# Cross-attention with LayerNorm: scaling on ScalarE, casts at the head of the next slot, projection six slots behind

## Chip, cores and metric

The kernel runs on one core of one Trainium2 chip. The metric is the device time of one execution in microseconds (us). Three runs of the kernel before took 683.48, 687.57 and 688.61 us; their median is 687.57.

## What is computed

A cross-attention layer with a residual and a LayerNorm. x is 4 x 2048 x 512, the context is 4 x 77 x 512, there are 16 heads of 32, all in f32; the mask is over the 77 context rows. Cut to what matters:

```python
qs = (q @ wq).reshape(Bq, Lq, H, HD).transpose(0, 2, 1, 3)
ks_ = (k @ wk).reshape(Bq, Lk, H, HD).transpose(0, 2, 1, 3)
vs = (v @ wv).reshape(Bq, Lk, H, HD).transpose(0, 2, 1, 3)
scores = jnp.einsum('bhqd,bhkd->bhqk', qs, ks_) / jnp.sqrt(jnp.float32(HD))
scores = jnp.where(mask[:, None, :, :], -jnp.inf, scores)
attn_w = jax.nn.softmax(scores, axis=-1)
attn = jnp.einsum('bhqk,bhkd->bhqd', attn_w, vs)
attn = attn.transpose(0, 2, 1, 3).reshape(Bq, Lq, H * HD)
out = attn @ wo + q
mu = jnp.mean(out, axis=-1, keepdims=True)
var = jnp.mean((out - mu) ** 2, axis=-1, keepdims=True)
return (out - mu) / jnp.sqrt(var + EPS) * gamma + beta
```

Here q is x, and k and v are both the context.

## The kernel before, in words

The 8192 rows of x are 64 tiles of 128 rows; two tiles make a block (32 blocks), sixteen tiles share one of the 4 batches of context. Every matmul on f32 data is made of three in a reduced format: each operand is split into a high part (a cast) and a low part (the difference), and high x high, high x low and low x high are added in PSUM. So every operand costs a cast on ScalarE and a subtraction on VectorE or GpSimd. The names of the parts end in h and l: xth and xtl (x, transposed), qh and ql (queries), ah and al (the values' product), kbh and kbl (keys, in blocks), wqh, wql, woh, wol (weights).

After a head that loads and splits the weights and makes the keys, a software pipeline runs over slots u = 0, 1, 2, ... (L423 on). The order of each engine's instructions is the order of the calls written out there by hand; no scheduler changes it. Every engine, and SP as the queue that issues most of the DMAs, works through its own list in order; tiles of a pool with so many buffers make an instruction wait until the buffer is free. In slot u, with tile t = u:

- load_xT (L108, odd slots): DMAs xT of a block, once on SP into xtf (one buffer) and once on GpSimd's queue into xth (two buffers). load_x (L325) brings the rows of tile u-4 for the residual.
- shift and scale (L359, L363, odd slots): for tiles u-7 and u-6, LayerNorm's -mean/std (L361, VectorE) and then the scaling of the even tile on VectorE (L371) and of the odd tile on ScalarE (L373).
- scores (L237): 12 matmuls (L248) into four PSUM banks, then 16 masked minimum operations on VectorE (L251), one a head, which write into pbuf (three buffers).
- exps (L262): 16 exponentials on ScalarE (L265), one a head, each with its sum.
- split_xT (L118, even slots) and affine (L375, odd slots), both on GpSimd: the low part of xT (L121), and gamma and beta of two tiles (L377, L378).
- transp (L282): VectorE transposes pbuf of tile u-1 in 32 x 32 blocks (L286). regroup (L291, even slots) has twelve DMAs of 128 KB, issued by SP (L297), which put the weights of a block into the order that the values' product wants (PT).
- mask_bias and mask_nan (L225, L230) for the next batch, in the thirteenth and fourteenth slot of each sixteen.
- o_proj (L329): 12 matmuls (L337) for tile u-5. av (L300, even slots): 32 small matmuls (L306), the product of values of block (u-4)/2. values (L177), in slots 1 to 3: the values themselves.
- q_half (L124): 24 matmuls (L138) for half of the queries of a later block.
- stats (L340): VectorE adds the projection and the residual (L343) into o (four buffers), takes the statistics (L345, L350, L356), and GpSimd the power -1/2 (L357).
- av_evac (L314, even slots): ScalarE casts ah (L320, two), VectorE subtracts al (L321). q_evac (L144): the same for qh (L148) and ql (L149).
- normalise (L274): VectorE's reciprocal of the sums (L277), and GpSimd's product with it (L280).
- store (L380, even slots): SP issues the two stores of tiles u-8 and u-7 (L381).

When a batch begins, kblocks (L168) casts the new keys on ScalarE (L173) and subtracts on VectorE (L174), between scores and exps. All PSUM tiles take turns in one pool of eight banks, in the order of the calls. The last four tiles are scaled on VectorE with gamma and beta in two operations (L368, L369).

Of the kernel before, what the change touches and what calls it, by code (L numbers as in the profile page):

```python
# [9 lines left out]
F32R = mybir.dt.float32r  # L10
# [3 lines left out]
ALU = mybir.AluOpType  # L14
# [3 lines left out]
P = 128  # L18
# [3 lines left out]
NK = 77  # L22
# [18 lines left out]
def xattn_layernorm(  # L41
# [43 lines left out]
    stage_b = sb.tile([P, 2, NC_D, D], F32, tag="PT", name="stage_b")  # L85
    ctx_t = sb.tile([P, NC_D, NB * NK], F32, tag="B", name="ctx_t")
    ctx_f = [ctx_t[:, c] for c in range(NC_D)]
    ctx_s = [sb.tile([P, NC_D, NB * NK], F32R, tag=t, name=f"ctx_s{t}") for t in ("AH", "AL")]
    wvh = [sb.tile([P, D], F32R, tag="o", bufs=4, name=f"wvh{c}") for c in range(NC_D)]
    wv2 = [sb.tile([P, 2, D], F32R, tag=t, name=f"wvl{t}") for t in ("AH", "AL")]  # L90
    wvl = [wv2[c // 2][:, c % 2] for c in range(NC_D)]
# [15 lines left out]

    def load_xT(b):  # L108
        f = sb.tile([P, NC_D, BLK], F32, tag="xtf", bufs=1, name=f"xtf_{b}")
        h = sb.tile([P, NC_D, BLK], F32R, tag="xth", name=f"xth_{b}")  # L110
        nc.sync.dma_start(f, xT[b])
        if b == 1:
            nc.scalar.copy(h, f)
        else:
            nc.gpsimd.dma_start(h, xT[b])
        blk[b] = [h, f]

    def split_xT(b):  # L118
# [49 lines left out]
    def kblocks(b, ms=slice(0, NG)):  # L168
        for j in range(GH):
            q = slice(HD * j, HD * (j + 1))  # L170
            cs = slice(NK * j, NK * (j + 1))
            src = kct[q, ms, b, keys_of(j)]
            nc.scalar.copy(kbh[q, ms, cs], src)  # L173
            nc.vector.tensor_tensor(kbl[q, ms, cs], src, kbh[q, ms, cs].bitcast(F32), ALU.subtract)  # L174


    def values(r0):  # L177
        w = min(P, NB * NK - r0)
        pv = bank(f"pv_{r0}")
        n = 0  # L180
        for c in range(NC_D):
            for i, v in ((0, wvh), (0, wvl), (1, wvh)):
                nc.tensor.matmul(
                    pv[:w, :], ctx_s[i][:, c, r0 : r0 + w], v[c], start=(n == 0), stop=(n == 11)
                )
                n += 1
        vt = sb.tile([P, D], F32, tag="xr", bufs=3, name=f"vt_{r0}")
        nc.scalar.copy(vt[:w], pv[:w])
        for b in range(NB):
            lo, hi = max(r0, b * NK), min(r0 + w, (b + 1) * NK)  # L190
            for a, k0, k1, p0 in ((0, 0, NK, 0), (1, 0, NK - TAIL_K, 0), (1, NK - TAIL_K, NK, NK)):
# [45 lines left out]
    def scores(t):  # L237
        b = t // 2
        qh, ql = qd[b]
        mb = bat[t // TPB][0]  # L240
        pb = pbuf[t % NPB]
        rs = slice((t % 2) * P, (t % 2) * P + P)
        nm = nmax[t] = sb.tile([P, H], F32, tag="nm", bufs=3, name=f"nm_{t}")
        sums[t] = sb.tile([P, H], F32, tag="sum", bufs=3, name=f"sum_{t}")
        for g in range(NG):
            sc = bank(f"sc_{t}_{g}")
            for n, (a, k) in enumerate(((qh, kbh), (qh, kbl), (ql, kbh))):
                nc.tensor.matmul(sc[:, :GW], a[:, g, rs], k[:, g, :], start=(n == 0), stop=(n == 2))  # L248
            for h in range(GH * g, GH * g + GH):
                j = h % GH  # L250
                nc.vector.tensor_tensor_reduce(  # L251
                    pb[:, h // 2, (h % 2) * NK : (h % 2 + 1) * NK],
                    sc[:, j * NK : (j + 1) * NK],
                    mb[:, t % TPB, keys_of(h)],
                    -1.0,
                    3.0e38,
                    ALU.add,
                    ALU.min,
                    accum_out=nm[:, h : h + 1],
                )  # L260

    def exps(t, lo, hi):  # L262
        pb = pbuf[t % NPB]
        for h in range(lo, hi):
            nc.scalar.activation(  # L265
                pb[:, h // 2, (h % 2) * NK : (h % 2 + 1) * NK],
                pb[:, h // 2, (h % 2) * NK : (h % 2 + 1) * NK],
                AF.Exp,
                bias=nmax[t][:, h : h + 1],
                scale=-1.0,  # L270
                accum_out=sums[t][:, h : h + 1],
            )
# [86 lines left out]
    def shift(b):  # L359
        mv, rn = mvs[b], rns[b]  # L360
        nc.vector.scalar_tensor_tensor(rn[:, 1, :], mv[:, :, 0], -1.0, rn[:, 0, :], ALU.mult, ALU.mult)  # L361

    def scale(t):  # L363
        o = od[t]
        b, tt = divmod(t, 2)
        mv, rn = mvs[b], rns[b]
        if t >= NT - TAILV:
            nc.vector.scalar_tensor_tensor(o, o, mv[:, tt, 0:1], gam, ALU.subtract, ALU.mult)  # L368
            nc.vector.scalar_tensor_tensor(o, o, rn[:, 0, tt : tt + 1], bet, ALU.mult, ALU.add)  # L369
        elif tt == 0:  # L370
            nc.vector.tensor_scalar(o, o, rn[:, 0, tt : tt + 1], rn[:, 1, tt : tt + 1], ALU.mult, ALU.add)  # L371
        else:
            nc.scalar.activation(o, o, AF.Identity, bias=rn[:, 1, tt : tt + 1], scale=rn[:, 0, tt : tt + 1])  # L373

    def affine(t):  # L375
        o = od[t]
        nc.gpsimd.tensor_tensor(o, o, gam, ALU.mult)  # L377
        nc.gpsimd.tensor_tensor(o, o, bet, ALU.add)  # L378

    def store(t):  # L380
        nc.sync.dma_start(out[t * P : (t + 1) * P, :], od.pop(t))  # L381
# [12 lines left out]
        nc.tensor.matmul(pw, warm[:, :P], warm, start=True, stop=True)  # L394

    x0f = sb.tile([P, NC_D, BLK], F32, tag="xtf", bufs=1, name="xtf_0")
    x0h = sb.tile([P, NC_D, BLK], F32R, tag="xth", name="xth_0")
    x0l = sb.tile([P, NC_D, BLK], F32R, tag="xtl", name="xtl_0")
    blk[0] = [x0h, x0l]
    for c in range(NC_D):  # L400
# [19 lines left out]
    mask_bias(0)  # L420
    mask_nan(0)


    load_xT(2)
    for u in range(NT + 9):
        t = u
        odd = u % 2
        b = (u + 5) // 2
        if odd and b < NBLK:
            load_xT(b)  # L430
        if 0 <= u - 4 < NT:
            load_x(u - 4)
        if odd and 0 <= u - 7 < NT - TAILV:
            shift((u - 7) // 2)
            scale(u - 7)
            scale(u - 6)
        if t < NT:
            scores(t)
            if t % TPB == TPB - 1 and t + 1 < NT:
                kblocks((t + 1) // TPB)  # L440
            exps(t, 0, 16)
        b = (u + 4) // 2
        if not odd and 2 <= b < NBLK:
            split_xT(b)
        if odd and 0 <= u - 7 < NT - TAILV:
            affine(u - 7)
            affine(u - 6)
        if 0 <= u - 1 < NT:
            transp(u - 1)
            if not odd:  # L450
                regroup((u - 1) // 2)
        m, at_ = divmod(u, TPB)
        if at_ == TPB - 6 and m + 1 < NB:
            load_mask(m + 1)
        if at_ == TPB - 4 and m + 1 < NB:
            mask_bias(m + 1)
        if at_ == TPB - 3 and m + 1 < NB:
            mask_nan(m + 1)
        o = u - 5
        if 0 <= o < NT:  # L460
            o_proj(o)
        b = (u - 4) // 2
        if not odd and 0 <= b < NBLK:
            av(b)
        if 1 <= u <= 3:
            values((u - 1) * P)
        qs = [(1, 0), (1, 1)] if u == 0 else [divmod(u + 3, 2)]
        qs = [q for q in qs if q[0] < NBLK]
        for q in qs:
            q_half(*q)  # L470
        if 0 <= o < NT:
            stats(o)
        if not odd and 0 <= b < NBLK:
            av_evac(b)
        for q in qs:
            q_evac(*q)
        if u == 0:
            load_wo()
        if 2 <= u <= 3:
            split_wo(2 * u - 4)  # L480
            split_wo(2 * u - 3)
        if t < NT:
            normalise(t)
        if o >= NT - TAILV and o < NT and (o % 2 or o >= NT - 2):
            for f in (o,) if o >= NT - 2 else (o - 1, o):
                scale(f)
                store(f)
        if not odd and 0 <= u - 8 < NT - TAILV:
            store(u - 8)
            store(u - 7)  # L490


# [43 lines left out]
```

## Time and profile before

| What | us |
|---|---|
| the profiled execution | 684.65 |
| its span | 682.9 |
| median of three runs | 687.57 |
| L265, exponentials on ScalarE, 1024 with their read-outs | 352.4 + 192.0, overlapping |
| L251, masked minimum on VectorE, 1024 with their read-outs | 164.7 + 82.0, overlapping |
| L138, query matmuls, 3 x 512 | 148.8 + 145.1 + 144.9 |
| L280, normalise on GpSimd, 64 | 144.8 |
| L286, transpose on VectorE, 64 | 96.5 |
| L373, scaling on ScalarE, 30 | 24.5 |

The mean granted clock of TensorE was 0.954 of full speed. How to read the lines of the profile: a group of instructions has its line in the kernel, the engine (PE is TensorE, DVE VectorE, ACT ScalarE, POOL GpSimd, SPq the queue of SP), the operation, what it writes and reads, the count, then the busy time in us and the mean duration in ns of one, and the idle time before. A wait has who waited for whom, the total in us, how often, and the longest. A line of a timeline has the start in us from the span's start, the duration in us, and then the instruction; what stands in brackets is the idle time ahead of it and who ended it. "issue" there means that nothing in the trace shows what it waited for. Matmuls are pipelined: their durations overlap, so the distance of two starts says what one costs.

### The profile page before, as it was taken

Reading aid. Unit: us, or ns where it says so; the run is one execution under the profiler, and the core shown is the slowest. Engines: PE = TensorE matmul, PEld = TensorE weight load, DVE = VectorE, ACT = ScalarE, POOL = GpSimd, SP = SyncE. Lnnn points to the kernel's source line nnn. Section 1 sums busy time; section 2 is a strip of 40 time slices with the busy share of each in tenths; the row PEclk is TensorE's granted clock in tenths of the full one; section 3 lists DMA queues with packets and bytes.
Section 4 is the critical chain, followed back from the end, with each engine's and each line's share of the span. In section 5 each row is a group of like instructions: output and inputs, shape, how many; then the busy total and the mean of one; then the engine's idle time right before and its main releaser. Section 6 shows DMA issues by size and latency. Waiting matters only on the chain.

```text
span 682.9 us, 15297 instructions
## 1 busy us (share of the span) xinstructions
PE 596.2 (87%) x4190; PEld 492.5 (72%) x4190; DVE 566.9 (83%) x2661; ACT 468.1 (69%) x2263; POOL 431.3 (63%) x303
## 2 busy tenths in 40 slices
PE   8996899988799888879699999998699989898754
PEld 6975788866687777668588787886588777676533
DVE  4666778899988889779988888889998888799936
ACT  6687766867767686676677777776866876677710
POOL 5662476766676676557576666775766677666641
PEclk9998999999999999999899999999899999999887
DMA  8646877665567765566756666677746666755652
GB/s 291 217 139 151 236 178 216 179 163 176 163 196 216 217 166 161 169 192 189 216 145 180 190 198 192 194 212 217 208 111 187 198 190 190 216 155 150 161 154 108
DMA packets 68463, 126.11 MB, mean 185 GB/s; under 512 B 14746, under 2 KB 16282, under 8 KB 68378
## 3 DMA queue, kind: packets, MB, share of 16 engines
q1 hardware_dynamic: 62954, 107.31, 55.3%
q0 software_dynamic: 5424, 17.83, 9.6%
q8 instruction: 34, 0.56, 0.3%
q14 instruction: 51, 0.42, 0.2%
HBM read 57.36 MB, written 16.78 MB: 109 GB/s over the span
## 4 chain that ended last, share of the span: by engine, by line
PE 31%; DVE 24%; ACT 20%; SPq 10%; DMA 7%; issue 5%; POOL 2%; POOLq 0%; DVEq 0%; ACTq 0%
ACT pbuf L265 17%; PE pq L138 11%; PE po L337 11%; SPq L297 9%; PE sc L248 6%; DMA out<-o 5%; DVE o L371 3%; DVE pbuf L251 3%; PE pa L306 3%; DVE ql L149 3%; DVE st L345 2%; DVE o L343 2%; DVE B L286 2%; DVE al L321 2%; DVE kbl L174 2%
## 5 line engine op out<-in xcount | busy, mean ns | idle before, releaser
L265 ACT ACTIVATE pbuf<-pbuf,nm 128x77 f32<-128x77 f32 x1024 | 352.4, 347 | 130.8 <-DVE nm L251 130.8
L280 POOL TENSOR_TENSOR pbuf<-pbuf,ri 128x1232 f32<-128x1232 f32 x64 | 144.8, 2262 | 158.9 <-DVE nm L251 97.3
L265 ACT ACTIVATION_READ_ACCUMULATOR pbuf<-pbuf,nm 128x1 f32 x1024 | 192.0, 188 | 0.0
L251 DVE CUSTOM_DVE_ANT_0 pbuf<-sc,mb 128x77 f32<-128x77 f32 x1024 | 164.7, 229 | 0.0
L138 PE MATMUL pq<-xth,wqh 128*128 128x256 f32 x512 | 148.8, 291 | 4.8 <-DVE ql L149 4.2
L138 PE MATMUL pq<-xtl,wqh 128*128 128x256 f32 x512 | 145.1, 283 | 1.8 <-POOL xtl L121 1.7
L138 PE MATMUL pq<-xth,wql 128*128 128x256 f32 x512 | 144.9, 283 | 0.5 <-DVE wql L98 0.4
L337 PE MATMUL po<-woh,ah 128*128 128x512 f32 x256 | 109.2, 427 | 33.1 <-ACT ah L320 27.7
L337 PE MATMUL po<-woh,al 128*128 128x512 f32 x256 | 108.9, 425 | 11.1 <-DVE al L321 11.1
L138 PEld LDWEIGHTS pq<-xth,wqh 128*128 128x128 f32 x512 | 98.1, 192 | 20.9 <-DVE ql L149 11.0
L337 PE MATMUL po<-wol,ah 128*128 128x512 f32 x256 | 105.9, 414 | 0.0
L286 DVE STREAM_TRANSPOSE B<-pbuf 128x1280 f32<-128x1280 f32 x64 | 96.5, 1507 | 5.7 <-POOL pbuf L280 5.6
L138 PEld LDWEIGHTS pq<-xtl,wqh 128*128 128x128 f32 x512 | 97.7, 191 | 3.9 <-POOL xtl L121 2.0
L138 PEld LDWEIGHTS pq<-xth,wql 128*128 128x128 f32 x512 | 97.7, 191 | 1.2 <-DVE wql L98 1.2
L248 PE MATMUL sc<-kbl,qh 128*128 128x308 f32 x256 | 80.0, 312 | 12.5 <-DVE kbl L174 12.5
L337 PEld LDWEIGHTS po<-woh,ah 128*128 128x128 f32 x256 | 51.6, 202 | 48.1 <-ACT ah L320 39.3
L343 DVE TENSOR_TENSOR o<-po,xr 128x512 f32<-128x512 f32 x64 | 43.0, 672 | 51.1 <-DMA out<-o 22.3
L121 POOL TENSOR_TENSOR xtl<-xtf,xth 128x1024 fp32r<-128x1024 f32 x31 | 74.5, 2404 | 16.0 <-DMA xtf<-xT 9.5
L251 DVE DVE_READ_ACCUMULATOR2_ANT nm<- 128x1 f32 x1024 | 82.0, 80 | 0.0
L248 PE MATMUL sc<-kbh,qh 128*128 128x308 f32 x256 | 79.8, 312 | 1.6 <-DVE nm L251 0.9
L378 POOL TENSOR_TENSOR o<-o,bet 128x512 f32<-128x512 f32 x60 | 77.9, 1298 | 4.7
L377 POOL TENSOR_TENSOR o<-o,gam 128x512 f32<-128x512 f32 x60 | 78.8, 1314 | 2.8 <-DVE o L371 2.2
(75 smaller groups left out, 944.1 us busy)
## 6 DMA issues: line engine op xcount, KB each, us to landing
PT<-B SPq DMA_DIRECT2D x384, 128.0 KB
xr<-x SPq DMA_DIRECT2D x64, 256.0 KB
out<-o SPq DMA_DIRECT2D x64, 256.0 KB
xtf<-xT SPq DMA_DIRECT2D x31, 512.0 KB
xth<-xT POOLq DMA_DIRECT2D x30, 512.0 KB, 4.7
stage_a<-wq SPq DMA_DIRECT2D x4, 256.0 KB
stage_a<-wk SPq DMA_DIRECT2D x4, 256.0 KB
stage_b<-wv SPq DMA_DIRECT2D x4, 256.0 KB
```

What stands on the lines that cost most here:

```text
L121: nc.gpsimd.tensor_tensor(l, f, h.bitcast(F32), ALU.subtract)
L138: nc.tensor.matmul(pq[:, i * BLK : (i + 1) * BLK], w[:, c, ms], r[:, c, :], start=(n == 0), stop=(n == 11))
L248: nc.tensor.matmul(sc[:, :GW], a[:, g, rs], k[:, g, :], start=(n == 0), stop=(n == 2))
L251: nc.vector.tensor_tensor_reduce(pb[:, h // 2, (h % 2) * NK : (h % 2 + 1) * NK], sc[:, j * NK : (j + 1) * NK], mb[:, t % TPB, keys_of(h)], ...
L265: nc.scalar.activation(pb[:, h // 2, (h % 2) * NK : (h % 2 + 1) * NK], pb[:, h // 2, (h % 2) * NK : (h % 2 + 1) * NK], AF.Exp, bias=nmax[t ...
L280: nc.gpsimd.tensor_tensor(pv, pv, rv.to_broadcast((P, NP, 2, NK)), ALU.mult)
L286: nc.vector.transpose(bts[b][:, :, :, tt, :].rearrange("p c q r -> p q c r"), pbuf[t % NPB].rearrange("p q (c r) -> p q c r", c=5),)
L297: nc.sync.dma_start(pt[32 * c : 32 * c + 32, i], src[32 * i : 32 * i + 32])
L337: nc.tensor.matmul(po, a[:, c, rs], w[:, c, :], start=(n == 0), stop=(n == 11))
L343: nc.vector.tensor_tensor(o, pos.pop(t), xr.pop(t), ALU.add)
L377: nc.gpsimd.tensor_tensor(o, o, gam, ALU.mult)
L378: nc.gpsimd.tensor_tensor(o, o, bet, ALU.add)
```

## The change

It does the following. Both tiles of a pair are scaled on ScalarE, and L371 is gone. The casts and subtractions of the queries and of the values' product leave the end of the slot and come at the head of the next one: behind the scores, ahead of kblocks, scale and exps. The projection runs six slots behind the scores instead of five, and what follows it moves along: loads of x at u-5, LayerNorm of tiles u-8 and u-7 in even slots, stores of tiles u-9 and u-8 in odd slots. Loads of xT come at the head of even slots and their splits in odd slots; split_xT(2) comes at the end of slot 0. xth has three buffers. The values are made in slots 1 (two parts) and 2 (one part) instead of 1, 2 and 3, and the split context that they and the keys read lies in the buffers with the tag B instead of AH and AL. mask_nan moves from the fourteenth to the fifteenth slot of sixteen.

```diff
-    ctx_s = [sb.tile([P, NC_D, NB * NK], F32R, tag=t, name=f"ctx_s{t}") for t in ("AH", "AL")]
+    ctx_2 = sb.tile([P, 2, NC_D, NB * NK], F32R, tag="B", name="ctx_s")
+    ctx_s = [ctx_2[:, i] for i in range(2)]
...
-        h = sb.tile([P, NC_D, BLK], F32R, tag="xth", name=f"xth_{b}")
+        h = sb.tile([P, NC_D, BLK], F32R, tag="xth", bufs=3, name=f"xth_{b}")
...
-        elif tt == 0:
-            nc.vector.tensor_scalar(o, o, rn[:, 0, tt : tt + 1], rn[:, 1, tt : tt + 1], ALU.mult, ALU.add)
         else:
             nc.scalar.activation(o, o, AF.Identity, bias=rn[:, 1, tt : tt + 1], scale=rn[:, 0, tt : tt + 1])
...
+    evac = []
...
-    for u in range(NT + 9):
-        t = u
+    for u in range(NT + 8):
         odd = u % 2
-        b = (u + 5) // 2
-        if odd and b < NBLK:
+        o = u - 6
+        b = (u + 6) // 2
+        if not odd and 3 <= b < NBLK:
             load_xT(b)
-        if 0 <= u - 4 < NT:
-            load_x(u - 4)
-        if odd and 0 <= u - 7 < NT - TAILV:
-            shift((u - 7) // 2)
-            scale(u - 7)
-            scale(u - 6)
-        if t < NT:
-            scores(t)
-            if t % TPB == TPB - 1 and t + 1 < NT:
-                kblocks((t + 1) // TPB)
-            exps(t, 0, 16)
-        b = (u + 4) // 2
-        if not odd and 2 <= b < NBLK:
-            split_xT(b)
-        if odd and 0 <= u - 7 < NT - TAILV:
-            affine(u - 7)
-            affine(u - 6)
+        if 0 <= u - 5 < NT:
+            load_x(u - 5)
+        ln = [f for f in (u - 8, u - 7) if not odd and 0 <= f < NT - TAILV]
+        if ln:
+            shift(ln[0] // 2)
+        if u < NT:
+            scores(u)
+        if odd and 0 <= (u - 5) // 2 < NBLK:
+            av_evac((u - 5) // 2)
+        for q in evac:
+            q_evac(*q)
+        if u < NT and u % TPB == TPB - 1 and u + 1 < NT:
+            kblocks((u + 1) // TPB)
+        for f in ln:
+            scale(f)
+        if u < NT:
+            exps(u, 0, 16)
         if 0 <= u - 1 < NT:
             transp(u - 1)
             if not odd:
                 regroup((u - 1) // 2)
...
+        b = (u + 5) // 2
+        if odd and 3 <= b < NBLK:
+            split_xT(b)
+        for f in ln:
+            affine(f)
...
-        if at_ == TPB - 3 and m + 1 < NB:
+        if k == TPB - 2 and m + 1 < NB:
             mask_nan(m + 1)
-        o = u - 5
         if 0 <= o < NT:
             o_proj(o)
         b = (u - 4) // 2
         if not odd and 0 <= b < NBLK:
             av(b)
-        if 1 <= u <= 3:
-            values((u - 1) * P)
-        qs = [(1, 0), (1, 1)] if u == 0 else [divmod(u + 3, 2)]
-        qs = [q for q in qs if q[0] < NBLK]
-        for q in qs:
+        for r in {1: (0, P), 2: (2 * P,)}.get(u, ()):
+            values(r)
+        evac = [(1, 0), (1, 1)] if u == 0 else [divmod(u + 3, 2)]
+        evac = [q for q in evac if q[0] < NBLK]
+        for q in evac:
             q_half(*q)
         if 0 <= o < NT:
             stats(o)
-        if not odd and 0 <= b < NBLK:
-            av_evac(b)
-        for q in qs:
-            q_evac(*q)
         if u == 0:
             load_wo()
+            split_xT(2)
...
-        if not odd and 0 <= u - 8 < NT - TAILV:
+        if odd and 0 <= u - 9 < NT - TAILV:
+            store(u - 9)
             store(u - 8)
-            store(u - 7)
```

More of the change, by code (lines that the diff above doesn't have):

```diff
@@ L396, in xattn_layernorm @@
     x0f = sb.tile([P, NC_D, BLK], F32, tag="xtf", bufs=1, name="xtf_0")
-    x0h = sb.tile([P, NC_D, BLK], F32R, tag="xth", name="xth_0")
+    x0h = sb.tile([P, NC_D, BLK], F32R, tag="xth", bufs=3, name="xth_0")
     x0l = sb.tile([P, NC_D, BLK], F32R, tag="xtl", name="xtl_0")
@@ L451, in xattn_layernorm @@
                 regroup((u - 1) // 2)
-        m, at_ = divmod(u, TPB)
-        if at_ == TPB - 6 and m + 1 < NB:
+        b = (u + 5) // 2
[3 more added lines that the diff above has]
+            affine(f)
+        m, k = divmod(u, TPB)
+        if k == TPB - 6 and m + 1 < NB:
             load_mask(m + 1)
-        if at_ == TPB - 4 and m + 1 < NB:
+        if k == TPB - 4 and m + 1 < NB:
             mask_bias(m + 1)
-        if at_ == TPB - 3 and m + 1 < NB:
+        if k == TPB - 2 and m + 1 < NB:
             mask_nan(m + 1)
-        o = u - 5
         if 0 <= o < NT:
@@ L481, in xattn_layernorm @@
             split_wo(2 * u - 3)
-        if t < NT:
-            normalise(t)
+        if u < NT:
+            normalise(u)
         if o >= NT - TAILV and o < NT and (o % 2 or o >= NT - 2):
```

## The prediction

> **What bounds the kernel now.** I read the busy shares of the page first, then the granted clock, the groups by cost, the waits, and last the timelines of two slots around 357 to 374 us.
>
> ```profile
> PE 596.2 (87%) x4190; PEld 492.5 (72%) x4190; DVE 566.9 (83%) x2661; ACT 468.1 (69%) x2263; POOL 431.3 (63%) x303
> ...
> L371 DVE TENSOR_SCALAR o<-o,rn 128x512 f32<-128x512 f32 x30 | 74.5, 2484 | 1.4
> ```
>
> No engine is full. The second line is the operation that the change takes off VectorE: 2.48 us, four times the 0.67 us of an addition of the same shape (L343). Its fastest instance took 0.545 us and most take 2.62 us, beside the 2.26 us of GpSimd's L280.
>
> ```profile
> ACT pbuf L265 <- DVE nm L251: 130.8, 63, 4.6
> ...
> ACT o L373 <- DVE rn L361: 41.1, 29, 6.0
> ...
> PE po L337 <- ACT ah L320: 27.7, 19, 3.7
> ...
> DVE o L343 <- DMA out<-o: 22.3, 9, 7.2
> ```
>
> ScalarE waits for VectorE in each of 63 slots, TensorE for ScalarE: a ring, not a full engine.
>
> ```profile
> 366.31 0.69 DVE L345 BATCH_NORM_STATS2 st<-o 128x6 f32<-128x512 f32 x1
> ...
> 367.25 0.16 DVE L356 TENSOR_TENSOR rn<-mv,nz 128x2 f32<-128x2 f32 x1
> 368.05 1.29 DVE L321 TENSOR_TENSOR al<-pa,ah 128x512 fp32r<-128x512 f32 x2 [0.64 <-ACT ah L320]
> 369.26 0.68 DVE L149 TENSOR_TENSOR ql<-pq,qh 128x512 fp32r<-128x512 f32 x1
> ...
> 370.16 2.63 DVE L371 TENSOR_SCALAR o<-o,rn 128x512 f32<-128x512 f32 x1
> ...
> 375.24 1.50 DVE L286 STREAM_TRANSPOSE B<-pbuf 128x1280 f32<-128x1280 f32 x1
> ```
>
> The same stretch on ScalarE:
>
> ```profile
> 367.45 1.05 ACT L320 CAST ah<-pa 128x512 fp32r<-128x512 f32 x2
> 368.40 0.58 ACT L148 CAST qh<-pq 128x512 fp32r<-128x512 f32 x1
> ...
> 373.03 0.36 ACT L265 ACTIVATE pbuf<-pbuf,nm 128x77 f32<-128x77 f32 x1 [2.06 <-DVE nm L251]
> ```
>
> ScalarE casts ah and qh only after its sixteen exponentials; VectorE waits for them, subtracts, scales for 2.63 us, and only then feeds the next exponentials, which start 5.6 us after the last ones ended.
>
> ```profile
> 357.22 0.30 PE L248 MATMUL sc<-kbh,qh 128*128 128x308 f32 x1
> ...
> 358.91 0.40 PE L337 MATMUL po<-woh,ah 128*128 128x512 f32 x1
> ...
> 361.80 1.93 PE L306 MATMUL pa<-PT,vsb 96*32 96x256 f32 x32
> ...
> 363.66 0.39 PE L138 MATMUL pq<-xth,wqh 128*128 128x256 f32 x1
> ...
> 366.58 0.30 PE L248 MATMUL sc<-kbh,qh 128*128 128x308 f32 x1
> ...
> 374.08 0.30 PE L248 MATMUL sc<-kbh,qh 128*128 128x308 f32 x1
> ```
>
> Here TensorE ran a pair of slots without a stall: 374.08 - 357.22 = 16.86 us. The mean pair is longer. Slots by the starts of L280: the eighth at 100.27, the last at 648.52; 548.25 us for 28 pairs, 19.58 each. Of the 2.7 us between them, L371 holds 2.6.
>
> ```profile
> 441.52 7.64 SPq L297 DMA_DIRECT2D PT<-B  x12
> ...
> 449.89 0.89 SPq L381 DMA_DIRECT2D out<-o  x2
> ```
>
> and on VectorE:
>
> ```profile
> 454.14 0.69 DVE L343 TENSOR_TENSOR o<-po,xr 128x512 f32<-128x512 f32 x1 [1.66 <-issue]
> ```
>
> A second limit lies in the odd slots: the store stands on SP behind twelve regrouping issues, lands some 3.3 us after its own issue ended, and VectorE's L343 needs the freed o buffer in the very next slot.
>
> **The change, part by part.**
>
> *Scaling.* Thirty L371 of 2.48 us leave VectorE (74.5 us); thirty more activations like L373 (0.82 us) join ScalarE. An even slot then holds two of them in a row; two casts overlap by about 0.1 us (1.05 for twice 0.575), so I take 1.55 us per pair of slots. The Trainium skill ("ScalarE: Activation LUTs", Rules for kernel authors) says to give multiplications and additions to VectorE, not ScalarE. Going by that rule and by VectorE's 0.545 us, this part would lose 28 x (0.82 - 0.55) = 8 us. The rows decide otherwise: with GpSimd busy the same operation holds VectorE 2.62 us.
>
> *Casts at the head.* Same counts: 64 L148, 64 L320 and their subtractions. On ScalarE they now stand ahead of the exponentials, so a new wait arises: qh waits for the query matmuls of the slot before, TensorE's last there, and two scalings and sixteen exponentials queue behind it. On VectorE al and ql follow the sixteen L251, ahead of the transpose and the statistics. I walk both rings, with starts from the rows above. Even slot: from L361 to the scaling 0.14 (370.01 to 370.15), two scalings 1.55, exponentials 5.50 (361.95 to 367.45), end and reciprocal 0.26: 7.45. Odd slot, on VectorE: L251 2.52, al 1.21, ql 0.60, transpose 1.43, addition 0.69, statistics 0.73 and 0.21, then L356, the power on GpSimd and L361, about 1.0 as that power is now awaited (L356 at 367.25; the power took 367.49 to 368.20): 8.4. Ring: 15.85 us per pair. TensorE: 16.86. So TensorE becomes the bound, by 1.0 us only. The wait of qh costs nothing while the exponentials end inside TensorE's slot: start of scores + 0.3 + 0.57 + 1.55 + 5.50 = 7.9 of 9.36 us in an even slot; if that cover of 1.4 us goes, the excess lengthens each pair. TensorE in turn waits for the moved subtractions: by the turn of the eight banks, the query matmuls of an odd slot take the bank that the first al frees, at about 0.65 + 2.52 + 0.6 = 3.8 us of the slot, and come at 1.7 + 2.9 = 4.6; in an even slot it is ql, 3.8 against 6.4. Both are hidden by 0.8 us or more.
>
> *Projection six slots behind.* ah and al are ready a slot early, so TensorE's waits for them go (27.7 + 11.1 us on PE); next to be late is its own order. The last slot to project is number 69 instead of 68. In the drain TensorE idles anyway (16.4 us busy of the 30 from 650 us on), the last value product keeps its place, and al then goes ahead of the statistics of tile 61 instead of behind: I take 0, between -1.5 and one more projection of 2.8.
>
> *Issues moved.* SP: the load of xT goes from the head of odd to the head of even slots, x one slot later; stores go from behind the regrouping of the even slot to the end of the odd slot after it (again behind that slot's regrouping), and L343 wants their buffer only after the next transpose, so transpose to landing is 7.64 + about 0.8 + 1.0 + 3.3 = 12.7 of now a full pair, 16.9. That second limit goes, with 4 us to spare. The regrouping has landed about 6.2 + 7.6 + 2.1 = 15.9 us after the even slot starts (2.1 from the last issue's end, 660.33, to the matmul at 662.47); its matmul comes at 16.9 + 4.6 = 21.5. On GpSimd the split of xT (2.4 us) changes to odd and the affine steps to even slots; its ring is power 0.72, normalise 2.26, issue of xth 0.62, four affine steps 5.4, normalise 2.26, transpose and statistics on VectorE 3.2: 14.5 of 16.9. xth (median 4.7 us to land) is issued 3.7 us into the even slot, the split wants it at about 11.8: 3.4 us of cover. Third xth buffer and ctx_s in tag B: no time of their own.
>
> *Batch switches, masks.* Three times TensorE stood 5.2 us for kbl, and then ran at half the clock: pitch 0.255 us instead of 0.14. The two slots around 341.65 took 23.2 us, 4 above a pair. kbl took 4.25 us beside the affine steps of GpSimd; in the new order GpSimd is about to wait for the power, and kbl falls between 0.4 and 4.25 us. VectorE has 1.0 of slack: 0 to 3.3 us each; I take 1.5, nearer the lower end, as GpSimd is mostly idle there. Masks (1.85 and 1.75 us) now both fall in even slots, where VectorE needs 6.2 of 7.45: under 0.7 us, three times each, inside the slack: 0.
>
> *Clock.* The granted clock fell to 0.83 between 420 and 430 us, where TensorE had idled 1.64 us; the projections then ran 0.43 instead of 0.23 us apart for 3.4 us. The Trainium skill ("TensorE: Matmul & The Clock Gate", What's actually happening) puts the drop after an idle window of about 3.4 us. By that page the new order never drops. By the row a gap of 1.6 us can be enough, at some 1.7 us each; I take none in steady slots and leave five (8 us) to the range.
>
> *Head.* Up to the eighth slot SP paces both: 16 issues of vsb (17.7 us) and two regroupings. The first value matmuls wait for the same landing near 72 us. 0, between -3 and +3.
>
> *Sum.* Pair: 16.86 plus two restarts of about 0.1 (a first matmul after a wait takes 0.39, not 0.28): 17.1. 28 x 17.1 + 3 x 1.5 = 483 for 548: -65. The profiled execution took 684.65 us (span 682.9), so 684.65 - 65 = 620. The median of the three runs, 687.57, is 2.9 higher; I stay with the profiled one.
>
> **Rivals.**
> *The ring stays the bound.* It has only 1.0 us of distance, with some ten hand-overs whose price in the new order I can't see; 0.2 to 0.3 each brings 17.9 to 18.9. At 18.2: 28 x 18.2 + 4.5 = 514, -34: 651. For it: 130.8 us of waits of ScalarE for VectorE. Against: the starts I summed contain the hand-overs.
> *The gain is hidden anyway.* If the late landings set the pair (regrouping issues took 8.97 instead of 7.64 us at 262.57, and DMA's busy share would rise from 0.66 to 0.77), it stays near 19.4: 28 x (19.58 - 19.4) = 5 less: 680. Against: 4 us of cover.
> *Slower.* L361 now stands at the head of VectorE's even slot and waits for the power, which on GpSimd stands behind the split of xT. If xth lands late, L361 holds all sixteen L251, the scalings and the exponentials. The split ends 3.3 us ahead of the power; 1.0 more is the ring's slack; to lose, a pair must pass 19.6, another 2.7. xth would need 4.7 + 3.4 + 3.3 + 1.0 + 2.7, near 15 us instead of 4.7, in nearly every pair; at 16.6, 1.5 us x 28 = 42 more: 727. For it: xT's landing was already waited for, twice, up to 5.8 us. Against: only twice in 31.
>
> **How the numbers follow.** TensorE the bound: 0.58, own range 605 (pair 16.86, head and drain 5 shorter) to 633 (five clock drops 8, switches at 3.3 each 5 more). Ring: 0.26, 633 to 668. Hidden: 0.07, near 680. Slower: 0.09. The range 605 to 662 holds the first and most of the second, 0.8. A measurement here tells 1% (7 us) from no change: faster 0.85, same 0.06, slower 0.09.
>
> **What would show it.** L371 gone and 60 activations at about 0.82; pairs of L280 near 17.1; TensorE above 91% busy with a clock above 0.97; no wait of L337 for ah, none of L343 for out; kbl under 2 us at the switches. Wrong, if ScalarE still waits over 2 us a slot for VectorE, if L148 at the head waits so long that exponentials end after TensorE's slot, or if L361 waits for the power more than 1 us.

## The result and the profile after

The changed kernel took 654.82 us (median of four runs, 654.69 to 655.74), the kernel before 688.09 (four runs, 683.48 to 689.30): a ratio of 0.953, 95% interval 0.949 to 0.958. The forecast was 620. So the change is faster, by about half of what was forecast, and the question is where the other 35 us are. Ratios leave out single runs that were more than 1.5% above the fastest of the same kernel: one of the nine with the scaling alone, and one of the kernel before beside it.

The page of the changed kernel (its helpers stand one line lower: L361 is L362 now, L280 is L281, L251 is L252; L373 is L372): the busy times, and the shares of lines in the chain that ended last.

```profile
PE 580.5 (89%) x4190; PEld 489.9 (75%) x4190; DVE 550.9 (84%) x2631; ACT 483.7 (74%) x2293; POOL 431.3 (66%) x303
...
DVE 53%; ACT 23%; PE 10%; issue 5%; POOL 4%; SPq 3%; DMA 2%; DVEq 0%; POOLq 0%; ACTq 0%
ACT pbuf L266 19%; DVE pbuf L252 12%; DVE rn L362 10%; DVE B L287 8%; DVE al L322 5%; PE pq L139 5%; DVE st L346 4%; POOL rn L358 4%; DVE o L344 3%; DVE ql L150 3%; ACT o L372 3%; SPq L298 2%; PE pa L307 1%; DVE kbl L175 1%; DVE nm L252 1%
...
L372 ACT ACTIVATE o<-o,rn 128x512 f32<-128x512 f32 x60 | 45.7, 808 | 106.9 <-DVE rn L362 106.9
```

Sixty activations of 0.81 us, as priced. But the chain is VectorE's and ScalarE's, not TensorE's, and third in it, with 10% of the span, stands L362: an operation on 128 x 2 numbers. The waits of the changed kernel (who waited for whom: total us, times, longest):

```profile
ACT o L372 <- DVE rn L362: 106.9, 30, 4.7
...
DVE rn L362 <- POOL rn L358: 20.1, 30, 0.8
...
ACT pbuf L266 <- DVE nm L252: 8.1, 4, 7.5
```

ScalarE's 130.8 us of waiting for the minima in 63 slots have become 106.9 us of waiting for L362 in 30. L362 itself waits only 0.67 us each for the power. The wait is not where the time is; the operation is. Its instances in the kernel before and in the changed one (min/median/max in ns):

```profile
L361 DVE SCALAR_TENSOR_TENSOR rn<-mv,rn x30: 94/96/148, 91.6 to 655.2; 128x2 f32<-128x2 f32 x30
```

```profile
L362 DVE SCALAR_TENSOR_TENSOR rn<-mv,rn x30: 160/2206/2212, 104.5 to 623.8; 128x2 f32<-128x2 f32 x30
```

The same instruction on the same 256 pairs of numbers took 0.096 us before and takes 2.2 us now. The timelines of a pair of slots show why. VectorE, changed kernel:

```profile
361.06 0.16 DVE L357 TENSOR_TENSOR rn<-mv,nz 128x2 f32<-128x2 f32 x1
361.14 0.24 DVE L278 RECIPROCAL ri<-sum 128x16 f32<-128x16 f32 x1
362.05 2.20 DVE L362 SCALAR_TENSOR_TENSOR rn<-mv,rn 128x2 f32<-128x2 f32 x1 [0.66 <-POOL rn L358]
...
371.34 0.25 DVE L278 RECIPROCAL ri<-sum 128x16 f32<-128x16 f32 x1 [1.01 <-ACT pbuf L266]
371.51 0.18 DVE L252 CUSTOM_DVE_ANT_0 pbuf<-sc,mb 128x77 f32<-128x77 f32 x1
...
373.98 1.28 DVE L322 TENSOR_TENSOR al<-pa,ah 128x512 fp32r<-128x512 f32 x2
...
377.21 0.65 DVE L344 TENSOR_TENSOR o<-po,xr 128x512 f32<-128x512 f32 x1
...
378.84 0.16 DVE L357 TENSOR_TENSOR rn<-mv,nz 128x2 f32<-128x2 f32 x1
...
379.83 2.21 DVE L362 SCALAR_TENSOR_TENSOR rn<-mv,rn 128x2 f32<-128x2 f32 x1 [0.67 <-POOL rn L358]
```

GpSimd and ScalarE in the same stretch:

```profile
361.30 0.71 POOL L358 TENSOR_TENSOR rn<-rn,mhalf 128x2 f32<-128x2 f32 x1 [2.78 <-DVE rn L357]
361.99 2.24 POOL L281 TENSOR_TENSOR pbuf<-pbuf,ri 128x1232 f32<-128x1232 f32 x1
```

```profile
364.29 1.52 ACT L372 ACTIVATE o<-o,rn 128x512 f32<-128x512 f32 x2 [3.36 <-DVE rn L362]
365.71 0.34 ACT L266 ACTIVATE pbuf<-pbuf,nm 128x77 f32<-128x77 f32 x1
...
371.21 1.04 ACT L321 CAST ah<-pa 128x512 fp32r<-128x512 f32 x2
```

The power ends at about 362.0 and releases L362. At the same moment GpSimd starts its next instruction, the normalise of 2.24 us, whose reciprocal has been ready since 361.4. L362 ends when the normalise ends; sixteen minima on VectorE, two scalings and sixteen exponentials on ScalarE stand behind it. The same place in the kernel before, GpSimd's rows and VectorE's in order of time:

```profile
367.49 0.71 POOL L357 TENSOR_TENSOR rn<-rn,mhalf 128x2 f32<-128x2 f32 x1 [0.96 <-DVE rn L356]
370.24 2.26 POOL L280 TENSOR_TENSOR pbuf<-pbuf,ri 128x1232 f32<-128x1232 f32 x1 [2.04 <-DVE rn L361]
```

```profile
369.86 0.24 DVE L277 RECIPROCAL ri<-sum 128x16 f32<-128x16 f32 x1
370.01 0.09 DVE L361 SCALAR_TENSOR_TENSOR rn<-mv,rn 128x2 f32<-128x2 f32 x1
370.16 2.63 DVE L371 TENSOR_SCALAR o<-o,rn 128x512 f32<-128x512 f32 x1
```

There the casts' subtractions and the reciprocal stood between L356 and L361, so the power was long done; L361 came directly behind the reciprocal, in 0.09 us, and the normalise started after it. Then it was L371 that ran beside the normalise, for 2.63 us. The change took L371 off VectorE and put L362 in its place.

The Trainium skill ("SBUF — State Buffer", Who interferes with whom) has the rule: a VectorE instruction with two inputs in SBUF contends with a GpSimd instruction that reads SBUF, and the later one blocks until the other has ended. L362 reads mv and rn, both there. The rows agree: 2.20 us beside 2.24 us, 0.096 without. They also show the price for an instruction this small: the other one's whole length.

### The profile page after: what moved, and what is told of

It reads as the page before. It is cut to its first block, busy times and chain, and to the rows that moved or that the text cites. A ratio compares the mean times of both kernels' runs of the same rounds, so it can differ in the third digit from the quotient of the medians.

```text
span 652.9 us, 15185 instructions
## 1 busy us (share of the span) xinstructions
PE 580.5 (89%) x4190; PEld 489.9 (75%) x4190; DVE 550.9 (84%) x2631; ACT 483.7 (74%) x2293; POOL 431.3 (66%) x303
## 4 chain that ended last, share of the span: by engine, by line
DVE 53%; ACT 23%; PE 10%; issue 5%; POOL 4%; SPq 3%; DMA 2%; DVEq 0%; POOLq 0%; ACTq 0%
ACT pbuf L266 19%; DVE pbuf L252 12%; DVE rn L362 10%; DVE B L287 8%; DVE al L322 5%; PE pq L139 5%; DVE st L346 4%; POOL rn L358 4%; DVE o L344 3%; DVE ql L150 3%; ACT o L372 3%; SPq L298 2%; PE pa L307 1%; DVE kbl L175 1%; DVE nm L252 1%
## 5 line engine op out<-in xcount | busy, mean ns | idle before, releaser
L266 ACT ACTIVATION_READ_ACCUMULATOR pbuf<-pbuf,nm 128x1 f32 x1024 | 194.9, 190 | 0.0
L281 POOL TENSOR_TENSOR pbuf<-pbuf,ri 128x1232 f32<-128x1232 f32 x64 | 144.0, 2251 | 55.5 <-DVE ri L278 51.0
L252 DVE CUSTOM_DVE_ANT_0 pbuf<-sc,mb 128x77 f32<-128x77 f32 x1024 | 164.9, 230 | 13.2 <-PE sc L249 13.2
L372 ACT ACTIVATE o<-o,rn 128x512 f32<-128x512 f32 x60 | 45.7, 808 | 106.9 <-DVE rn L362 106.9
L338 PE MATMUL po<-woh,ah 128*128 128x512 f32 x256 | 106.7, 417 | 7.5 <-DVE o L344 5.6
L338 PE MATMUL po<-woh,al 128*128 128x512 f32 x256 | 105.4, 412 | 2.5 <-DVE al L322 2.5
L358 POOL TENSOR_TENSOR rn<-rn,mhalf 128x2 f32<-128x2 f32 (+1 forms) x33 | 24.5, 743 | 111.7 <-DVE rn L357 111.7
L249 PE MATMUL sc<-kbl,qh 128*128 128x308 f32 x256 | 78.2, 305 | 6.7 <-DVE kbl L175 6.7
L307 PE MATMUL pa<-PT,vsb 96*32 96x256 f32 x1024 | 65.3, 398 | 19.9 <-DMA vsb<-vt 14.5
L252 DVE DVE_READ_ACCUMULATOR2_ANT nm<- 128x1 f32 x1024 | 82.3, 80 | 0.0
```

Source lines behind the costliest of these rows:

```text
L252: nc.vector.tensor_tensor_reduce(pb[:, h // 2, (h % 2) * NK : (h % 2 + 1) * NK], sc[:, j * NK : (j + 1) * NK], mb[:, t % TPB, keys_of(h)], ...
L266: nc.scalar.activation(pb[:, h // 2, (h % 2) * NK : (h % 2 + 1) * NK], pb[:, h // 2, (h % 2) * NK : (h % 2 + 1) * NK], AF.Exp, bias=nmax[t ...
L281: nc.gpsimd.tensor_tensor(pv, pv, rv.to_broadcast((P, NP, 2, NK)), ALU.mult)
L307: nc.tensor.matmul(pas[b][g // 2][HD * j : HD * (j + 1), (g % 2) * BLK : (g % 2 + 1) * BLK], vsb[:, 2 * b // TPB, HD * h : HD * (h + 1)], ...
L338: nc.tensor.matmul(po, a[:, c, rs], w[:, c, :], start=(n == 0), stop=(n == 11))
```

## The experiments

Theory: L362 meets the normalise, and that is most of what is missing; without it a pair is bound by TensorE, as forecast. Rivals: the ring is slow from many small hand-overs; TensorE is bound by something else; the moves that the order brings (head, tail) took the gain. All times below are medians, with the ratio to the kernel before run beside them (688.4 to 691.1). "Pair" is the distance of normalise starts over two slots.

### Another instruction of GpSimd between power and normalise

```diff
+    def load_xh(b):
+        xhs[b] = sb.tile([P, NC_D, BLK], F32R, tag="xth", bufs=3, name=f"xth_{b}")
+        nc.gpsimd.dma_start(xhs[b], xT[b])
...
+        if odd and 4 <= (u + 7) // 2 < NBLK:
+            load_xh((u + 7) // 2)
```

The DMA issue of xth moves from the head of the even slot to the end of the odd one, ahead of normalise.

> The changed kernel with one edit: GpSimd issues the DMA of xth (0.62 us) between the power and the normalise of an odd slot instead of after that normalise; no operation is added or removed. Theory (collision): L362 takes 2.2 us only because the normalise, 2.24 us long, starts on GpSimd at the same moment. With the issue between them L362 takes about 0.1 us, VectorE's and ScalarE's even slot starts 1.9 us earlier, the ring falls from 17.78 to about 15.9 us a pair, and TensorE's 16.8 to 16.9 is next: 28 pairs x 0.9 = 25 less, with some slack for masks and keys 628 us, between 622 and 635. Rival (hand-overs: the ring is longer by many small delays and L362's duration only shows a wait that something else would take over): no less than 648. If the issue itself holds VectorE as the normalise does, L362 takes about 0.6 and the time is still near 630.

618.80 us (617.87 to 621.40), ratio 0.899 (0.894 to 0.903), 3 us below the lower end of what was expected. GpSimd and VectorE of this run (L364 is the power, L368 the old L362):

```profile
343.05 0.71 POOL L364 TENSOR_TENSOR rn<-rn,mhalf 128x2 f32<-128x2 f32 x1 [2.32 <-DVE rn L363]
343.72 0.62 POOL L123 DMA_DIRECT2D xth<-xT  x1
344.36 2.27 POOL L287 TENSOR_TENSOR pbuf<-pbuf,ri 128x1232 f32<-128x1232 f32 x1
```

```profile
343.79 0.16 DVE L368 SCALAR_TENSOR_TENSOR rn<-mv,rn 128x2 f32<-128x2 f32 x1 [0.66 <-POOL rn L364]
```

The wait for the power is the same 0.66 us, the operation 0.16 instead of 2.20: nothing but the place of that one issue was changed, and 36 us went. The instances of L368 over the whole run still hold a few collisions:

```profile
L368 DVE SCALAR_TENSOR_TENSOR rn<-mv,rn x30: 160/161/2854, 107.2 to 590.1; 128x2 f32<-128x2 f32 x30
```

Four of them make the comparison once more inside this one execution: behind the last load of xT there is no issue left to stand between, L368 takes 2.2 us again (at 528.14, 545.90, 563.66 and 580.81), and the pairs are 17.76, 17.76 and 17.15 us, as at the end of the changed kernel (17.74, 17.76 and 17.16). The longest, 2.85 us at 107.17, stays unexplained.

### The operation itself on GpSimd

```diff
             nc.gpsimd.tensor_tensor(rn[:, 0, j], rn[:, 0, j], mhalf[:, j], ALU.pow)
+            if t < NT - TAILV:
+                nc.gpsimd.tensor_tensor(rn[:, 1, :], mv[:, :, 0], rn[:, 0, :], ALU.mult)
+                nc.gpsimd.tensor_tensor(rn[:, 1, :], rn[:, 1, :], mone, ALU.mult)
...
-        if ln:
-            shift(ln[0] // 2)
```

> The changed kernel with L362 taken off VectorE: GpSimd multiplies the mean by the result of the power and then by -1, two products of 128x2, straight behind the power, ahead of the normalise. Theory (collision): VectorE's even slot starts right after its reciprocal; the scalings start when the two small products end, 0.2 to 1.5 us after the power instead of 2.3; pair at TensorE's 16.9 where they are short, 17.2 where they take 0.7 each as the power does: 628 to 640 us, taken 631. Rival (hand-overs): within 1% of 655.

607.96 us (606.82 to 608.21), ratio 0.882 (0.878 to 0.886). GpSimd, then ScalarE, then the busy times:

```profile
337.77 0.71 POOL L359 TENSOR_TENSOR rn<-rn,mhalf 128x2 f32<-128x2 f32 x1 [2.13 <-DVE rn L358]
338.56 0.20 POOL L361 TENSOR_TENSOR rn<-mv,rn 128x2 f32<-128x2 f32 x1
338.83 0.19 POOL L362 TENSOR_TENSOR rn<-rn,mone 128x2 f32<-128x2 f32 x1
338.98 2.25 POOL L282 TENSOR_TENSOR pbuf<-pbuf,ri 128x1232 f32<-128x1232 f32 x1
```

```profile
339.06 1.52 ACT L376 ACTIVATE o<-o,rn 128x512 f32<-128x512 f32 x2 [1.67 <-POOL rn L362]
```

```profile
PE 562.7 (93%) x4190; PEld 479.0 (79%) x4190; DVE 492.2 (81%) x2601; ACT 484.1 (80%) x2293; POOL 440.8 (73%) x364
```

The two products take 0.195 us each and VectorE, without L362, goes straight on to the minima. The time is 20 us below the lower end of what was expected. Between 100 and 300 us TensorE is busy for 199.4 of 200 us in this run and for 198.9 in the one before it: now TensorE is the bound. Its pair, from one values' product to the next, is 16.73 us there (178.36 to 195.09) and 16.44 us here (174.37 to 190.82).

### The even tile's scaling back on VectorE

```diff
+        elif tt == 0:
+            nc.vector.tensor_scalar(o, o, rn[:, 0, tt : tt + 1], rn[:, 1, tt : tt + 1], ALU.mult, ALU.add)
...
             shift(ln[0] // 2)
+            scale(ln[0])
```

> The changed kernel with the scaling of the even tile back on VectorE, right behind L362, ahead of the scores; ScalarE scales the odd tile only. Theory (collision; an even slot is set by the chain L362, scalings, exponentials): when L362 ends, the normalise has ended too, so the scaling takes VectorE 0.55 us, not 2.6; ScalarE has one scaling of 0.73 us less ahead of its exponentials, and these start 0.2 to 0.65 us earlier: 637 to 650 us, taken 643. So moving the scaling would be no gain in this order. Rival (the scaling's move to ScalarE is what brought the gain): 2 us longer in each pair, 655 + 56 = 711.

647.17 us (645.65 to 648.03), ratio 0.939 (0.935 to 0.943).

```profile
L372 DVE TENSOR_SCALAR o<-o,rn 128x512 f32<-128x512 f32 x30 | 16.4, 546 | 1.1
```

In the new order the scaling follows L362, which has already sat out the normalise, so VectorE does it in 0.546 us and ScalarE is spared 0.8: the pair is 17.23 instead of 17.78 us, 0.55 shorter, or 15 us over 28 pairs. The two pairs at a switch of the batch give some of it back (19.1 and 21.4 us instead of 18.9 and 21.0). In the new order the move of the scaling costs time.

### Casts and subtractions back at the end of the slot

```diff
-        if odd and 0 <= (u - 5) // 2 < NBLK:
-            av_evac((u - 5) // 2)
-        for q in evac:
-            q_evac(*q)
...
             stats(o)
+        if not odd and 0 <= b < NBLK:
+            av_evac(b)
+        for q in evac:
+            q_evac(*q)
```

Lag of six, both scalings on ScalarE and the moved loads stay.

> The changed kernel with its casts and subtractions (L321, L149, L322, L150) back at the end of the slot, as in the kernel before; scaling on ScalarE and the projection six slots behind stay. Theory (collision): L362 is then reached after ScalarE's casts, the power is over and the normalise has not begun, so L362 takes 0.1 us; against that the casts stand in the ring again. Ring: shift and scalings 1.65, exponentials 5.5, three casts 1.55, subtraction and reciprocal 0.85 in the even slot, 9.6; 7.4 in the odd slot; pair 17.0 against 17.78: 28 x 0.8 = 22 less, 633 us, between 628 and 645. Rival (moving the casts is what brought the gain): slower than the changed kernel, 665 to 690.

630.50 us (630.08 to 631.12), ratio 0.912 (0.909 to 0.916). VectorE, GpSimd and the instances of L362:

```profile
350.44 0.69 DVE L150 TENSOR_TENSOR ql<-pq,qh 128x512 fp32r<-128x512 f32 x1 [0.63 <-ACT qh L149]
351.05 0.24 DVE L278 RECIPROCAL ri<-sum 128x16 f32<-128x16 f32 x1
351.21 0.10 DVE L362 SCALAR_TENSOR_TENSOR rn<-mv,rn 128x2 f32<-128x2 f32 x1
```

```profile
349.89 0.71 POOL L358 TENSOR_TENSOR rn<-rn,mhalf 128x2 f32<-128x2 f32 x1 [0.96 <-DVE rn L357]
351.44 2.25 POOL L281 TENSOR_TENSOR pbuf<-pbuf,ri 128x1232 f32<-128x1232 f32 x1 [0.83 <-DVE rn L362]
```

```profile
L362 DVE SCALAR_TENSOR_TENSOR rn<-mv,rn x30: 96/97/2201, 107.3 to 600.0; 128x2 f32<-128x2 f32 x30
```

With ql and the reciprocal between L357 and L362 the power is done in time, and the normalise waits for the reciprocal that stands directly ahead of L362 (the profile names L362, which ends at the same moment within 0.02 us). Moving the casts, as it was done, lost 24 us. Against the first two runs its pair is about as short (16.76 us), but a switch of the batch still costs it 4.2 us (a pair of 20.99). The four subtractions of kbl span 4.21 us there, beside GpSimd's split of xT (2.40 us), where they span 2.36 in the first run above. So with L362 out of the way the order with the casts at the head is the shorter one, and what shows of it is at the switches.

### Lag of six alone

Casts as in the run above, and the even tile's scaling on VectorE behind L362.

```diff
+        elif tt == 0:
+            nc.vector.tensor_scalar(o, o, rn[:, 0, tt : tt + 1], rn[:, 1, tt : tt + 1], ALU.mult, ALU.add)
...
             shift(ln[0] // 2)
+            scale(ln[0])
...
-        for f in ln:
+        for f in ln[1:]:
             scale(f)
```

> The changed kernel with casts and subtractions back at the end of the slot and the scaling of the even tile back on VectorE behind L362: of the change, the projection six slots behind (with the loads, stores and splits that move along) and the edits in the head remain. Theory (collision): L362 takes 0.1, then the scaling on VectorE meets the normalise as in the kernel before and takes 2.6 us; exponentials start 2.9 us behind L362 instead of 1.6; pair 16.77 + 1.3 = 18.1: 630.5 + 28 x 1.3 = 667 us, between 655 and 675. So with the casts at the end the scaling's move to ScalarE is a gain, with the casts at the head (647 against 655) it is none, by what GpSimd does at that moment. Rival (the scaling on VectorE is better in either order): under 630.

671.92 us (671.17 to 672.82), ratio 0.978 (0.975 to 0.981), pair 18.22. VectorE:

```profile
352.21 0.10 DVE L362 SCALAR_TENSOR_TENSOR rn<-mv,rn 128x2 f32<-128x2 f32 x1
352.36 2.62 DVE L372 TENSOR_SCALAR o<-o,rn 128x512 f32<-128x512 f32 x1
```

L362 is short and the scaling is held instead, 2.62 us, as before the change. Beside the run above, only the place of the scaling differs: there taking it off VectorE gained 41 us; in the order of the changed kernel it lost 8.

### The scaling alone, in the old order

```diff
-        elif tt == 0:
-            nc.vector.tensor_scalar(o, o, rn[:, 0, tt : tt + 1], rn[:, 1, tt : tt + 1], ALU.mult, ALU.add)
```

> The kernel before with one edit: both tiles of a pair are scaled on ScalarE; casts, the five slots of the projection, loads and stores stay. Theory: VectorE loses 2.6 us in the odd slot, but the exponentials start only 1.3 us earlier, behind two scalings, and the odd slot is also held by the store that L343 waits for (transpose to landing 12.5 us): 0 to 1.3 us a pair, 655 to 690, taken 672. Rival (VectorE's 2.6 us are the whole of the distance to TensorE's pair): 2.6 x 28 = 73 less, 615.

683.82 us (nine runs, 679.15 to 690.94), ratio 0.993 (0.989 to 0.998). At a lag of five the scaling off VectorE gains 0.7%, at a lag of six 6%, though L361 takes 0.10 us in both. The lag of six alone gains 16 us, the scaling alone 4 to 5, both together 58: each of the two pays little while the other limit stands. In the profiled execution (690.94 us, the longest of the nine) L343 waits 27.0 us for stores, 21.2 for loads of x and 21.8 for nothing that the trace shows, against 22.3, 3.8 and 10.7 in the kernel before. That fits the late landings of the prediction's second limit, but what holds the pairs in the old order was not tested further.

### Head and tail

Three runs on the changed kernel. One loads the fifth block of xT ahead of the values' DMAs:

```diff
-        if not odd and 3 <= b < NBLK:
+        if not odd and 3 <= b < NBLK and b != 4:
             load_xT(b)
...
+        if u == 1:
+            load_xT(4)
```

> The changed kernel with one edit in the head: the load of xT's fifth block is issued on SP and GpSimd ahead of the values' thirteen DMAs of slot 1 instead of behind them in slot 2. Theory: in the changed kernel the split of that block waited 11.4 us for its load and held the normalise of the fourth slot, and the eighth normalise came at 104.45 instead of 100.27. With the edit the split's wait goes and 1.5 to 4 us with it: 652 us. Rival (SP's issues of vsb set the head whatever stands between): 655.

654.63 us (654.30 to 655.23), ratio 0.950 (0.945 to 0.955): nothing gained, and the eighth normalise starts at 105.43 instead of 104.45 us. One puts the second part of the values back behind the first regrouping:

```diff
-        for r in {1: (0, P), 2: (2 * P,)}.get(u, ()):
+        for r in {1: (0,), 2: (P, 2 * P)}.get(u, ()):
```

> The changed kernel with one edit in the head: the second part of the values is made in slot 2, behind the first regrouping, instead of in slot 1, so that five instead of thirteen issues of vsb stand ahead of that regrouping on SP. Theory: in the changed kernel the first values' product waited until 75.05 us for its operands; in the kernel before it began at 62.3 us with five issues ahead. With the edit it begins near 63 us and the eighth normalise comes 3 to 5 us earlier: 651 us. Rival (all sixteen issues and two regroupings set the head in any order): 654 to 655.

654.68 us (653.47 to 655.86), ratio 0.947 (0.944 to 0.951). The first values' product came at 65.85 instead of 75.1 us, but GpSimd's split of the next block then waited for its load, which stands behind the values' issues on SP:

```profile
79.53 2.40 POOL L122 TENSOR_TENSOR xtl<-xtf,xth 128x1024 fp32r<-128x1024 f32 x1 [12.56 <-DMA xtf<-xT]
```

The eighth normalise starts at 104.3 instead of 104.45 us, no difference: in the next run, whose head is that of the changed kernel, it starts at 105.5. One sends the projection of tile 61 ahead of the last values' product:

```diff
-        if 0 <= o < NT:
-            o_proj(o)
+        for p in {NT - 4: (NT - 4, NT - 3), NT - 3: ()}.get(o, (o,)):
+            if 0 <= p < NT:
+                o_proj(p)
```

> The changed kernel with one edit in the drain: the projection of tile 61 is called ahead of the last values' product instead of behind it. Theory: from the last normalise to the end the changed kernel takes 38.4 us, the kernel before 34.4, because a third projection stands behind the last values' product, at half the clock: 4.3 us. With the edit 3 to 4 us go: 651 us. Rival (the drain is set by SP's loads and stores): 654 to 655.

653.32 us (651.99 to 655.57), ratio 0.946 (0.942 to 0.949). The stretch behind the last normalise is 37.4 us, beside 38.4 in the changed kernel and 38.0 in the two runs above, which have the same drain: a gain of 0.5 to 1 us, and the times of the whole kernel overlap. Next in line VectorE waits for an o buffer that a store has not freed:

```profile
633.64 0.69 DVE L344 TENSOR_TENSOR o<-po,xr 128x512 f32<-128x512 f32 x1 [8.59 <-DMA out<-o]
```

### The best of these together

L362 on GpSimd, the second part of the values in slot 2, the projection of tile 61 early (the diffs above).

> The changed kernel with three edits together: L362's work on GpSimd behind the power, the second part of the values in slot 2, tile 61's projection ahead of the last values' product. Theory: 608 of the first edit alone less 4 for the head and 3.5 for the drain: 600 us. Rival (head and drain overlap with what the shorter ring already set free): 608.

604.24 us (603.04 to 607.52), ratio 0.875 (0.871 to 0.879): the lowest median, though its range overlaps that of the run with only L362 on GpSimd. Beside that run the eighth normalise is 1.7 us earlier (103.79), little more than the 1 us by which equal heads differ, and the tail 2.9 shorter (35.9).

## Why the prediction was wrong, point by point

- **The step that failed: "from L361 to the scaling 0.14".** It was read off the old timeline (370.01 to 370.15), where L361 met nobody. In the pair of the changed kernel shown above it is 2.24 us (362.05 to 364.29). Every other term of the ring held: two scalings 1.42 (1.55), exponentials 5.50 (5.50), their end to the minima 0.30 (0.26), minima 2.47 (2.52), al, ql and transpose 3.23 (3.24), addition and statistics 1.63 (1.63), L357 to the start of L362 0.99 (1.0). They sum to 17.78 us instead of 15.85, so the ring passes TensorE's pair, and "TensorE becomes the bound" fails with it. The prediction had ordered both neighbours (the power ends, then the normalise starts) for GpSimd's own ring, but did not put L361 beside them.
- **The test for it looked at the wrong column.** "L361 waits for the power more than 1 us" stayed false, at 0.67. The loss is in the duration of L362. Nor did "ScalarE still waits over 2 us a slot" show on the mean: 106.9 + 8.1 us over 64 slots are 1.8 each, but it is 3.6 in every even slot. What was to be seen if TensorE were the bound did not come: TensorE was 89% busy, not above 91%, its clock 0.955, not above 0.97, pairs took 17.78, not near 17.1, and kbl 2.35 us, not under 2.
- **What a pair cost.** 17.78 instead of 17.1: 28 x 0.68 = 19 us. The switches of the batch: the masks make one pair 18.88, kbl and the masks the next 21.00, 4.3 us together where 1.5 was taken: 3 x 2.8 = 8. They had been priced with 1.0 of slack between the ring and TensorE's pair, and a ring without that slack passes on what it can't hide itself: 1.1 of the 2.2 us of mask operations in an even slot, where VectorE idles 1.01 us. kbl itself fell between its bounds of 0.4 and 4.25:

```profile
320.04 2.35 DVE L175 TENSOR_TENSOR kbl<-kct,kbh 32x308 fp32r<-32x308 f32 x4
```

  In the two runs without the collision eight pairs with a switch are 0.7 and 1.0 us above eight of TensorE's pairs.
- **The clock** was taken without a drop in steady slots, and there it held: 1.00 from 195 to 245 and from 341 to 440 us. Once a batch TensorE stood 1.84 to 1.88 us for L344, behind the mask operations on VectorE; over 3.5 us from half a microsecond later on, the granted clock was 0.51, 0.54 and 0.58, and projections ran 0.43 us apart. The three gaps of 1.57 and 1.58 us at the switches left it at 1.00. So the row's reading held, that a gap well under 3.4 us can be enough. In these slots VectorE sets the pace; the time that the drops cost was not separated.
- **Head and tail, taken at 0:** the eighth normalise came 4.2 us later (104.45 for 100.27) and the stretch behind the last took 38.4 instead of 34.4. Both are outside their bounds. Of the tail, the place of the one projection explains 0.5 to 1 us; VectorE's long wait for a store there (6.3 us near 630) does not explain the difference, since the old order had one of 7.2 at the same place. Of the head it is shown that with two other orders of SP's issues the eighth normalise comes at the same time or later. What makes the rest of either stays open. 19 + 8 + 4.2 + 4.0 makes the 35 us.
- **What was right.** TensorE's pair without a stall, 16.86 us, was a good bound: 16.73 in the run with the DMA issue between, whose 618.8 us is close to the forecast of 620 (its pairs, 16.89 in the mean, are shorter than the 17.1 taken, its head and tail 12 longer together: the closeness of the two times is in part luck). L371 is gone and an activation costs 0.81; TensorE waits for ah once (1.8 us) instead of 19 times; the second limit, the late stores, is gone from steady slots and outside the switches and the last three the pairs run from 17.77 to 17.80 us, where they ran from 18.6 to 20.8 before; qh at the head waits 9.3 us in all.
- **Two readings of the old trace** were off as well. "Of the 2.7 us between them, L371 holds 2.6": with L371 gone and nothing else changed, 4 to 5 us went, where 2.6 in each of 28 pairs would be 73. And "three times TensorE stood 5.2 us for kbl": the three waits sum to 12.5 us, and 5.2 is the longest.
- **The rivals.** "The ring stays the bound" gave 651, and the ring did. But its reason, some ten hand-overs of 0.2 to 0.3 us each, is refuted: they cost what was summed, and one collision of 2.1 us a pair made the difference. So its 651 came near by another cause. "The gain is hidden anyway" and "Slower" are refuted by the shorter, equal pairs and by the 0.67 us; "Slower" had looked at the right place, L361 at the head of VectorE's even slot, but for a late start and not for its own length.
- **The rule weighed at the scaling** (the Trainium skill, "ScalarE: Activation LUTs", Rules for kernel authors: multiplications and additions to VectorE) was set aside because of the 2.62 us beside GpSimd. Both can be seen here: with the casts at the end and a lag of six, setting it aside gained 41 us; in the changed order, where VectorE needs 0.546 us, following it gains 8. That the prediction worked out 8 by the rule is a coincidence: it took 0.27 us a pair, and the pair gained 0.55, of which the switches took back a part.

| Casts and subtractions | even scaling on | the operation of L361, now L362 | us |
|---|---|---|---|
| before, lag of five | VectorE | 0.10, then the scaling 2.62 | 688 |
| before, lag of five | ScalarE | 0.10 | 684 |
| end of slot, lag of six | VectorE | 0.10, then the scaling 2.62 | 672 |
| end of slot, lag of six | ScalarE | 0.10 | 630 |
| head of next slot | VectorE | 2.2 | 647 |
| head of next slot (the change) | ScalarE | 2.2 | 655 |
| head of next slot, DMA issue between | ScalarE | 0.16 | 619 |
| head of next slot | ScalarE | on GpSimd | 608 |
| the same, head and tail edits | ScalarE | on GpSimd | 604 |

## What to carry to other kernels

Price an instruction by what runs beside it in the new order, not by its row in the old one: when an operation of VectorE with two inputs in SBUF is released by the end of a GpSimd instruction, ask what GpSimd starts at that same moment, however small the operation is. Look at durations as well as at waits, since a collision of this kind shows as a long instruction, and the waits in the profile are those of the engines behind it. And if it sits on the ring, a half-microsecond instruction put between the two can be worth more than the change itself: here 36 us against 33.

## What the runs showed of the hardware that was not expected

- An instruction of VectorE on 128 x 2 numbers took as long as the GpSimd instruction beside it: 2.20 us beside 2.24 us. A DMA issue on GpSimd (0.62 us) did not hold it: 0.16 us.
- A product of 128 x 2 on GpSimd took 0.195 us, the power of the same shape 0.71.
- TensorE's matmuls are not equally dense in all orders, at a clock of 1.00 in both runs from 100 to 300 us: 24 query matmuls took 2.82 and 2.96 us in the two slots of a pair of the first run above, 2.74 and 2.85 in the one with L362 on GpSimd. Why is open.
